# Two attention layers on one core: output products move to step 6, the first value products to step 7, and a weight copy moves between ScalarE's copy and VectorE's addition

## The chip, the core and the metric

The kernel runs on one core of a Trainium2 chip. The metric is the time of one execution on the device, in microseconds (us), lower is better. Before the change the median of three runs is 3574.42 us (3573.12 to 3576.17). The profiled execution has a span of 3577.0 us, with a granted TensorE clock of 0.994 of full speed, so throttling plays no part.

## What is computed

Four images of 32 x 32 positions with 768 channels go through two layers. Each layer normalizes in 32 groups, runs 12-head attention (head size 64) with decomposed relative position biases, projects, and adds the result to its input. All of it is fp32. Cut to one layer:

```
S = 32*32; hd = 64
q, k, v = split(groupnorm(x) @ Wqkv)              # 12 heads, [S, hd] each
bias    = rel_h[q_row, k_row] + rel_w[q_col, k_col]   # both are products of q with a small table
attn    = softmax(scale * q @ k.T + bias)         # [S, S] for each head and image
out     = (attn @ v) @ Wproj + bproj
x       = x + out
```

## The kernel before

**Pairs and steps.** Work is cut into 48 pairs of heads: 2 layers x 4 images make 8 images, each with 6 pairs (`pair` 0 to 5; the text counts pairs through, 0 to 47). A pair has 8 steps, `n` = 0 to 7, one for each block of 128 queries. The order of every engine's instructions is written out by hand in the main loop (L709 to L794): [...].

**What a step does.** In step n the loop issues, for the next block of queries, the score products (`scores`, L475 on TensorE: both heads, 1024 keys). VectorE then takes scores and bias together (L484) into a tile `sc`; ScalarE takes the exponential (L488). For the block of the step itself, already exponentiated, `turn` (L515) lets VectorE transpose 32 x 32 blocks into a tile `tb`. Then `divide` (L495, L499, L501) scales the next block by the inverse of its sums. GpSimd adds the two bias parts for the block after (L461).

**The way through DRAM.** Two steps fill one quarter of the queries. After each odd step SyncE writes `tb` to DRAM (`td<-tb`, L518, 1 MB for each head), and `read_back` (L526, `pt<-td`, 1 MB for each head) brings it back in the layout that the value products need. The first quarter (written in step 1) is read back in step 3, the second (step 3) in step 4, the third (step 5) in step 7, the fourth (step 7) in step 0 of the next pair. There are three `tb` buffers for the two heads together and two `pt` buffers for each head.

**Value products.** `weigh` (L545, `av<-pt,v`) multiplies two quarters with the values: quarters 0 and 1 in step 6 of the pair, quarters 2 and 3 in step 2 of the next pair. They need `pt` to have landed, and their end frees `pt` buffers.

**Filling work.** `take` hands out groups of matmuls that prepare the next pair or finish an earlier image: `project_in` (L268, four units a pair), `project_values` (L376), `project_out` (L621, four products a pair, three groups each). `shares` says how many groups each step takes. Before the change the four output products stand in step 7, and step 6 has no share, because the value products are there. An output product needs its weights (`wo`, L580) and the tile that it is added to (`res`, L600), which `fetch` loads half in step 4, half in step 6.

**PSUM.** All of the filling work, the position products (`tp`, L408) and the value products share one pool `ps_m` of two tiles. A product can start when the product two before it has been taken out of PSUM by VectorE or ScalarE. Scores have a pool of their own, one tile for each head.

**Saved products.** For pairs that are not `plain` (L237: the first pair of an image and pair 1 are plain) some products of `project_in` are saved with sums of weights: `sum_weights` (L318: one ScalarE copy L324, three GpSimd operations L327 to L329) runs in steps 6 and 7 two pairs ahead. In unit 0, `sum_weights_last` (L333) has VectorE overwrite part of `w0` (L336, 64x384) and GpSimd the rest (L337). Unit 1, three groups in step 1, reads what L336 wrote. `sum_input` (L339) prepares sums of the inputs on GpSimd in the last pair of each image.

**SyncE's queue.** Nearly all transfers are issued by SyncE, in order; [...]. In the built program each transfer also waits until the one eight before it has landed.

Of the kernel before, what the change touches and what calls it, by code (L numbers as in the profile page):

```python
# [52 lines left out]
NT = S // P  # L53
# [5 lines left out]
NP = NH // 2  # L59
FULL = 2 * HW - 1  # L60
BIG = 3.0e38
NX, NY = 2 * NC, NC + NC // 2
# [4 lines left out]
def attention_blocks(ctx: ExitStack, tc: tile.TileContext, a: dict, out: bass.AP):  # L67
# [28 lines left out]
    NPAIR = NI * NP  # L96
# [24 lines left out]
    def load_w(g, which):  # L121

        im, pair = divmod(g, NP)
        if which == 2:
            w = wpool.tile([P, NC, 2 * P], FP, tag="wv", name=f"wv_{g}")
            src = a[f"wv{images[im][0]}"][pair // 2]
        else:
            w = wpool.tile([P, NC, P], FP, tag=f"w{which}", name=f"w_{g}_{which}")
            src = a[f"wqk{images[im][0]}"][pair, which]
        w_of[g, which] = w  # L130
        nc.sync.dma_start(out=w, in_=src.rearrange("p (c o) -> p c o", c=NC))
# [105 lines left out]
    def plain(g):  # L237
        return g % NP == 0 or g == 1

    def add(to, t, x, bias=None):  # L240

        if bias is None:
            nc.vector.tensor_tensor(to, t, x, ALU.add)  # L243
        else:
            nc.vector.scalar_tensor_tensor(to, t, bias, x, ALU.add, ALU.add)

    def project_in(g, unit):

        im, pair = divmod(g, NP)
        xs, ys = x_of[im], y_of[im]  # L250
        if unit == 0:
            for which in range(2):
                tag = "qk"[which]
                qk_of[g, which] = qkpool.tile([P, S], FP, tag=tag, name=f"{tag}_{g}")
        if plain(g):
            which, i = divmod(unit, 2)
            w, x = 2 * [w_of[g, which]], xs[i * NC : (i + 1) * NC]
        else:
            w0, w1, w3 = w_of[g, 0], w_of[g, 1], w_of[g, 3]
            w, x = (  # L260
                ((w0, w0), xs[:NC]), ((w0, w3[:, 3:]), ys[NC:]),
                ((w3, w0), xs[NC:]), ((w1, w1), ys[:NC]),
            )[unit]
        t = ps_m.tile([P, 2, HALF], FP, tag="m", name=f"pj_{g}_{unit}")
        for c in range(len(x)):
            for a in range(2):
                rows = slice(a * D, (a + 1) * D)
                nc.tensor.matmul(  # L268
                    t[:, a, :], lhsT=w[a][rows, c, :], rhs=x[c][rows, :],
                    start=(c == 0), stop=(c == len(x) - 1),  # L270
                )
            if c < len(x) - 1:
                yield True

        q = [
            qk_of[g, 0][:, i * HALF : (i + 1) * HALF].rearrange("p (m a) -> p m a", a=4)
            for i in range(2)
        ]
        k = qk_of[g, 1].rearrange("p (a m) -> p a m", a=4)
        k = [k[:, :, i * P : (i + 1) * P] for i in range(2)]  # L280
        u = [t[:, a, :].rearrange("p (m a) -> p m a", a=4) for a in range(2)]
        t = [x.rearrange("p m a -> p a m") for x in u]
        bias = [None, None]
        if images[im][0]:
            bias = [bqkv[:, which, pair : pair + 1] for which in range(2)]
        if plain(g):
            to = k[i]
            if which == 0:
                to, t = q[i], u
            if images[im][0] == 0:  # L290
                nc.scalar.copy(to, t[0])
            else:
                nc.scalar.activation(to, t[0], AF.Identity, bias=bias[which])
            add(to, t[1], to)
        elif unit == 0:
            nc.scalar.copy(k[0], t[0])
            add(q[0], u[1], k[0].rearrange("p a m -> p m a"), bias[0])
            sum_weights_last(g)
        elif unit == 1:
            add(k[0], t[0], k[0])  # L300
            add(k[0], t[1], k[0])
        elif unit == 2:
            add(k[1], t[0], k[0])
            add(q[1], u[1], k[1].rearrange("p a m -> p m a"), bias[0])
        else:
            add(k[1], t[0], k[1], bias[1])
            add(k[0], t[0], k[0], bias[1])
            nc.vector.tensor_tensor(k[0], k[0], t[1], ALU.subtract)
        if unit in ((0, 1) if plain(g) else (0, 2)):
            (later if g else mid).append(lambda: positions(g, 1 if unit else 0))  # L310
        if g + 1 < NPAIR:
            if unit == (1 if plain(g) else 2):
                later.append(lambda: load_w(g + 1, 0))
            if unit == 3:
                early.append(lambda: load_w(g + 1, 1))
        yield True
# [16 lines left out]
    def sum_weights_last(g):  # L333

        w0, w3 = w_of[g, 0], w_of[g, 3]
        nc.vector.tensor_copy(w0[TOP, :3], w3[LOW, :3])  # L336
        nc.gpsimd.tensor_tensor(w0[LOW], w0[LOW], w3[LOW], ALU.subtract)  # L337

    def sum_input(im, n):  # L339

        xs, ys = x_of[im], y_of[im]

        def each(chunks):
            return [(c, xs[c], xs[NC + c], ys[c], ys[NC + c % 3], TOP if c < 3 else LOW) for c in chunks]

        sub = lambda out, x, y: nc.gpsimd.tensor_tensor(out, x, y, ALU.subtract)  # L346
        for c, a, b, y, z, half in each({-1: (0, 1, 2), 0: (3,), 1: (4,), 2: (5,)}.get(n, ())):
            nc.scalar.copy(y[LOW], b[TOP])  # L348
            sub(y[TOP], b[LOW], y[LOW])
        for c, a, b, y, z, half in each({1: (0,), 2: (1, 2), 3: (3,), 4: (4, 5)}.get(n, ())):  # L350
            nc.gpsimd.tensor_tensor(z[half], y[TOP], a[TOP], ALU.add)  # L351
            if half == TOP:
                nc.scalar.copy(y[LOW], z[TOP])
        for c, a, b, y, z, half in each({5: (0,), 6: (1, 2), 7: (3, 4, 5)}.get(n, ())):
            sub(b[TOP], b[TOP], a[TOP])
        for c, a, b, y, z, half in each({9: (0, 1, 2), 10: (3, 4, 5)}.get(n, ())):
            sub(y[LOW], (y if half == TOP else z)[LOW], a[LOW])
# [291 lines left out]
    early, mid, later, last, behind, behind2 = [], [], [], [], [], []  # L649
# [32 lines left out]
    with tc.manual_schedule(engines=ENGINES):  # L682
# [26 lines left out]
        for at, (g, n) in enumerate(units):  # L709
            im, pair = divmod(g, NP)  # L710
            end = im + 1 == NI
            if n == 0:
                shares = [6, 6, 0, 6, 12, 6, 0, 12] if g + 1 >= NPAIR or plain(g + 1) else [6, 9, 0, 6, 6, 6, 0, 12]
                ins = (todo if at == 0 else []) + prepare(g + 1)
                if pair < 3:
                    if at == 0:
                        shares = [12, 6, 0, 6, 12, 6, 0, 0]
                    todo = ins + (put_out(im - 1, 1, range(4 * pair, 4 * pair + 4)) if im else [])
                elif pair < NP - 1:
                    todo = ins + put_out(im, 0, range(4 * pair - 12, 4 * pair - 8))  # L720
                    if pair == 3 and not end:
                        stages, apply = norm(im + 1)
                else:
                    todo = ins + put_out(im, 0, range(8, 12))
                    if end:
                        fetch_last()
                        todo += put_out(im, 1, range(12)) + put_out(im, 2, range(0, 12, 2))
                        shares = [6, 6, 0, 6, 6, 2, 0, 4]
# [8 lines left out]
            early, later = later, early  # L737

            upto = 4 * (pair % 3) + 3
            if n in (4, 6) and (im, pair) >= (0, 3):  # L740
                upto -= 6 - n
                fetch(place[((im, 0) if pair >= 3 else (im - 1, 1)) + divmod(upto, 2)])

            ask = [divmod(g + 3, NP)] if n == 1 else []
# [14 lines left out]
            if pair == 3 and n in stages and not end:  # L759
                stages[n]()  # L760
            share = shares[n]
            first = 3 if n == NT - 1 else 2 if end and pair == NP - 1 and n in (3, 4) else 0
            first = min(first, share)
            take(todo, first)
            share -= first
# [1 line left out]
            if at + 1 < len(units):  # L767
                divide(*units[at + 1])
            if pair == 4 and not end:
                for c in {2: (0, 1), 4: (2, 3), 6: (4, 5, 6, 7), 7: range(8, NX)}.get(n, ()):  # L770
                    if n == 7 and c % 2 == 0:
                        take(todo, 3)
                        share -= 3
                    apply(c % NC, c // NC)
            if g + 2 < NPAIR and not plain(g + 2) and n in (6, 7):
                if n == 6:
                    combine = sum_weights(g + 2)
                combine[n - 6]()
            take(todo, share)
            if last:  # L780
                last.pop(0)()
            if pair == NP - 2 and n == 7 and not end:
                sum_input(im + 1, -1)
# [4 lines left out]
            elif g == 0:  # L788
                for k in (-1, 0) if n == 0 else (n,):
                    sum_input(0, k)  # L790
            if n == 6:
                weigh(g, (0, 1))
            elif n == 2 and g:
                weigh(g - 1, (2, 3))  # L794
# [62 lines left out]
```

## Time and profile before

| | before |
|---|---|
| time, median of 3 | 3574.42 us |
| TensorE (PE) busy | 3417.6 us, 96% |
| VectorE (DVE) busy | 2592.0 us, 72% |
| GpSimd (POOL) busy | 2492.1 us, 70% |
| ScalarE (ACT) busy | 1986.2 us, 56% |
| DMA, queue 1 | 1020.53 MB, 79.3% of 16 engines' span |
| one transposition on VectorE (L515) | 768 of 1222 ns |
| one output product's removal from PSUM (L632; L630) | 680 ns; 741 ns |
| weight copy on VectorE (L336) | 39 of 647 ns |
| ScalarE's copy of k in unit 0 (L296) | 39 of 566 ns |
| VectorE's addition of queries (L243 q; L245 q) | 38 of 1065 ns; 40 of 1121 ns |
| GpSimd weight sums (L327, L328, L329, L337) | 39 each of about 1805 ns |

The first rows are shares of the span; the lower rows are groups of instructions with their count and mean duration. The page also gives the time that an engine was idle just before a group, and what ended the idle time. TensorE's 3577.0 - 3417.6 = 159.4 us of idle time can thus be put down to what it waited for. A timeline lists one engine's instructions in order, with the start in us from the span's start, the time from the first start to the last end of a run of equal instructions, and in brackets the idle time before it with its releaser.

### The profile page before, as it was taken

What the parts mean: (1) busy time and instruction counts of PE and PEld (TensorE: products, weight loads), DVE (VectorE), ACT (ScalarE), POOL (GpSimd) and SP (SyncE); (2) the same over time, 40 slices, a digit from 0 to 9 for tenths busy, and PEclk for the clock granted to TensorE, in tenths of its full rate; (3) what the DMA queues carried; (4) which work ended last, traced back from release to release, by engine and by line L of the source; (5) the groups of instructions that cost most, each with busy time, mean ns of one, the idle gap of its engine ahead of it and who ended that gap; (6) DMA issues with size and microseconds to landing.
All of it is one profiled execution on the core that took longest, in us unless ns stands there. A gap on an engine that the chain in (4) does not pass through costs nothing.

```text
span 3577.0 us, 56189 instructions
## 1 busy us (share of the span) xinstructions
PE 3417.6 (96%) x20652; PEld 1897.0 (53%) x20652; DVE 2592.0 (72%) x4011; ACT 1986.2 (56%) x3958; POOL 2492.1 (70%) x1510
## 2 busy tenths in 40 slices
PE   6899999999999999999999999999999999999999
PEld 4455555555555556555555555555555555555554
DVE  4687867777777777777777777777766677776776
ACT  3565565555555556555655566555654555555552
POOL 3877686676967669676786667876678666786663
PEclk9999999999999999999999999999999999999999
DMA  3688978888788887888888788878988789887878
GB/s 118 244 287 319 328 278 302 318 309 316 276 316 317 300 307 272 319 293 306 292 308 304 281 316 301 306 285 292 308 307 301 271 290 330 299 291 276 296 288 289
DMA packets 531220, 1051.55 MB, mean 294 GB/s; under 512 B 143872, under 2 KB 206848, under 8 KB 481792
## 3 DMA queue, kind: packets, MB, share of 16 engines
q1 hardware_dynamic: 476448, 1020.53, 79.3%
q10 hardware_dynamic: 54496, 27.43, 2.6%
q8 instruction: 162, 2.65, 0.3%
q14 instruction: 114, 0.93, 0.1%
HBM read 572.73 MB, written 475.10 MB: 293 GB/s over the span
## 4 chain that ended last, share of the span: by engine, by line
PE 52%; DVE 17%; DMA 15%; ACT 5%; issue 5%; POOL 4%; SPq 2%; ACTq 0%; DVEq 0%; POOLq 0%
PE pj L268 13%; PE av L545 12%; PE s L475 10%; PE o L621 10%; DVE tb L515 8%; DMA td<-tb 7%; DMA pt<-td 7%; PE pv L376 6%; DVE sc L484 5%; ACT sc L501 2%; PE tp L408 2%; POOL sc L461 2%; DVE x L228 1%; POOL x L346 1%; POOL x L351 1%
## 5 line engine op out<-in xcount | busy, mean ns | idle before, releaser
L461 POOL TENSOR_TENSOR sc<-rel,rel 128x1024 f32<-128x1024 f32 x768 | 1546.1, 2083 | 42.6 <-DMA rel<-tdr 35.8
L488 ACT ACTIVATE sc<-sc,sm 128x1024 f32<-128x1024 f32 x768 | 880.1, 1147 | 662.8 <-DVE sm L484 660.0
L499 POOL TENSOR_SCALAR sc<-sc,sm 128x1024 f32<-128x1024 f32 x384 | 435.5, 1134 | 934.4 <-DVE sm L495 926.4
L484 DVE CUSTOM_DVE_ANT_0 sc<-s,sc 128x1024 f32<-128x1024 f32 x768 | 908.7, 1220 | 214.1 <-PE s L475 164.9
L268 PE MATMUL pj<-x,w 64*128 64x512 f32 x4140 | 938.7, 598 | 99.3 <-DVE w L336 60.1
L515 DVE STREAM_TRANSPOSE tb<-sc 128x1024 f32<-128x1024 f32 x768 | 913.0, 1222 | 122.9 <-DMA td<-tb 122.8
L545 PE MATMUL av<-pt,v 128*64 128x256 f32 x6144 | 717.3, 385 | 41.0 <-DMA pt<-td 41.0
L475 PE MATMUL s<-k,q 64*128 64x512 f32 x3072 | 746.3, 596 | 6.2 <-DVE sm L484 6.1
L501 ACT ACTIVATE sc<-sc,sm 128x1024 f32<-128x1024 f32 x384 | 441.0, 1148 | 556.8 <-DVE sm L495 556.8
L268 PEld LDWEIGHTS pj<-x,w 64*128 64x128 f32 x4140 | 415.7, 189 | 600.2 <-issue 444.4
L545 PEld LDWEIGHTS av<-pt,v 128*64 128x64 f32 x6144 | 446.0, 138 | 341.4 <-DMA pt<-td 60.3
L376 PE MATMUL pv<-wv,x 64*128 64x256 f32 x4608 | 514.1, 376 | 0.0
L376 PEld LDWEIGHTS pv<-wv,x 64*128 64x128 f32 x4608 | 446.4, 187 | 92.2 <-issue 29.9
L621 PE MATMUL o<-attn,wo 128*128 128x512 f32 x1080 | 480.5, 598 | 8.5 <-DVE attn L554 3.5
L475 PEld LDWEIGHTS s<-k,q 64*128 64x128 f32 x3072 | 289.2, 187 | 297.0 <-issue 272.7
L431 ACT COPY rel<-t 32x64 f32<-32x64 f32 x1504 | 362.9, 241 | 15.4
L621 PEld LDWEIGHTS o<-attn,wo 128*128 128x128 f32 x1080 | 199.9, 190 | 285.9 <-issue 234.4
L418 ACT COPY t<-tp 128x512 f32<-128x512 f32 x188 | 110.0, 585 | 191.5 <-PE tp L408 137.0
L243 DVE TENSOR_TENSOR k<-pj,k 128x512 f32<-128x512 f32 x173 | 116.8, 684 | 136.8 <-PE pj L268 94.9
L346 POOL TENSOR_TENSOR x<-x,x 64x512 f32<-64x512 f32 x144 | 182.6, 1288 | 43.9 <-ACT x L348 28.8
L391 DVE TENSOR_TENSOR v<-pv,v 128x256 f32<-128x256 f32 x192 | 81.4, 424 | 91.2 <-ACT v L388 88.0
L488 ACT ACTIVATION_READ_ACCUMULATOR sc<-sc,sm 128x1 f32 x768 | 143.2, 187 | 0.0
(54 smaller groups left out, 1516.9 us busy)
## 6 DMA issues: line engine op xcount, KB each, us to landing
td<-tb SPq DMA_DIRECT2D x384, 1024.0 KB, 5.6
pt<-td SPq DMA_DIRECT2D x382, 1024.0 KB, 8.0
w<-in_wqk SPq DMA_DIRECT2D x96, 384.0 KB, 3.5
tdr<-t ACTq DMA_DIRECT2D x94, 256.0 KB, 4.6
x<-in_x SPq DMA_DIRECT2D x84, 256.0 KB, 6.6
part<-res SPq DMA_DIRECT2D x84, 256.0 KB, 5.5
res<-part SPq DMA_DIRECT2D x84, 256.0 KB, 6.9
wv<-in_wv SPq DMA_DIRECT2D x24, 768.0 KB, 12.1
```

The lines of the kernel that those rows point to most:

```text
L268: nc.tensor.matmul(t[:, a, :], lhsT=w[a][rows, c, :], rhs=x[c][rows, :], start=(c == 0), stop=(c == len(x) - 1),)
L376: nc.tensor.matmul(t[:, a, k, :], lhsT=xs[i // 2 * NC + c][rows, at * P : (at + 1) * P], rhs=w[rows, c, :], start=(c == 0), stop=(c == NC ...
L431: nc.scalar.copy(rel[of, :, j, :], t[of, j, :, at : at + HW])
L461: nc.gpsimd.tensor_tensor(sc.rearrange("p (a k) (u l) -> p a l (k u)", a=4, l=8), rel0[:, h, :].unsqueeze(1).unsqueeze(2).to_broadcast(shape),
L475: nc.tensor.matmul(ps[h][:, cols], lhsT=q[rows, n * P : (n + 1) * P], rhs=k[rows, cols], start=True, stop=True,)
L484: nc.vector.tensor_tensor_reduce(out=sc, in0=ps[h], in1=sc, scale=-scale, scalar=BIG, op0=ALU.add, op1=ALU.min, accum_out=st[:, 0, h : h + 1],
L488: nc.scalar.activation(sc, sc, AF.Exp, bias=st[:, 0, h : h + 1], scale=-1.0, accum_out=st[:, 1, h : h + 1],)
L499: nc.gpsimd.tensor_scalar(sc, sc, st[:, 2, h : h + 1], 1.0, ALU.mult, ALU.mult)
L501: nc.scalar.activation(sc, sc, AF.Copy, scale=st[:, 2, h : h + 1])
L515: nc.vector.transpose(tb[:, :, j, :], sc_of[g, n, h])
L545: nc.tensor.matmul(av[rows, at * 2 * P : (at + 1) * 2 * P], lhsT=v_of[g][:, k, rows], rhs=pt_of[g, quarter, h][:, :, k, :], start=(k == 0) ...
L621: nc.tensor.matmul(t, lhsT=wo_of[im, o, c], rhs=attn_of[im * NP + c, i], start=(c == c0), stop=(c == c1 - 1),)
```

## The change

Three things move, and some timing around them is adapted.

1. In unit 0 of `project_in`, the weight copy (L336) and GpSimd's subtraction are issued before VectorE's addition of queries instead of after it, so that VectorE can do the copy while ScalarE still copies k.
2. The four output products move from step 7 to step 6; from pair 3 to pair 46 (`late`) the value products of quarters 0 and 1 move from step 6 to step 7. This gives the second quarter's read-back more time. `fetch` accordingly loads both `wo` tiles and all four `res` tiles in step 5.
3. `sum_weights` runs one step earlier (5 and 6) unless the next pair is plain; two rows of the position bias copies (`rows_axis`, L431) are allowed in step 3; the normalization of the next image's inputs (`apply`, L228) is spread differently over the steps of pair 4; `sum_input` is one step earlier in places.

```diff
         elif unit == 0:
             nc.scalar.copy(k[0], t[0])
+            sum_weights_last(g)
             add(q[0], u[1], k[0].rearrange("p a m -> p m a"), bias[0])
-            sum_weights_last(g)
...
-        for c, a, b, y, z, half in each({5: (0,), 6: (1, 2), 7: (3, 4, 5)}.get(n, ())):
+        for c, a, b, y, z, half in each({5: (0, 1), 6: (2, 3, 4, 5)}.get(n, ())):
...
-                shares = [6, 6, 0, 6, 12, 6, 0, 12] if g + 1 >= NPAIR or plain(g + 1) else [6, 9, 0, 6, 6, 6, 0, 12]
+                shares = [6, 6, 0, 6, 12, 6, 12, 0] if g + 1 >= NPAIR or plain(g + 1) else [6, 9, 0, 6, 6, 6, 12, 0]
+                late = g > 2 and g + 1 < NPAIR
...
-            if n in (4, 6) and (im, pair) >= (0, 3):
-                upto -= 6 - n
+            if n == 5 and (im, pair) >= (0, 3):
                 fetch(place[((im, 0) if pair >= 3 else (im - 1, 1)) + divmod(upto, 2)])
...
-            first = 3 if n == NT - 1 else 2 if end and pair == NP - 1 and n in (3, 4) else 0
+            first = 3 if n == (6 if late else 7) else 2 if end and pair == NP - 1 and n in (3, 4) else 0
...
-                for c in {2: (0, 1), 4: (2, 3), 6: (4, 5, 6, 7), 7: range(8, NX)}.get(n, ()):
-                    if n == 7 and c % 2 == 0:
+                for c in {2: (0, 1), 3: (2,), 4: (3,), 5: (4,), 6: range(5, 10), 7: (10, 11)}.get(n, ()):
+                    if n == 6 and c % 2 == 0:
...
-            if g + 2 < NPAIR and not plain(g + 2) and n in (6, 7):
-                if n == 6:
+            if g + 2 < NPAIR and not plain(g + 2):
+                k = n - (6 if plain(g + 1) else 5)
+                if k == 0:
                     combine = sum_weights(g + 2)
-                combine[n - 6]()
+                if k in (0, 1):
+                    combine[k]()
...
-            if last:
+            for k in range(min(len(last), 2 if n == 3 else 1)):
                 last.pop(0)()
...
-            if n == 6:
+            if n == (7 if late else 6):
                 weigh(g, (0, 1))
```

## The prediction

> **What bounds the kernel now.** I read the shares first: TensorE is busy in 96% of the span, VectorE in 72%. So only TensorE's gaps can be won, and any delay elsewhere counts only where TensorE comes to wait for it. Its waits name the gaps (us in total, times, longest):
>
> ```profile
> PE pj L268 <- DVE w L336: 60.1, 39, 4.4
> PE av L545 <- DMA pt<-td: 41.0, 34, 2.7
> PE pj L268 <- DVE x L228: 25.8, 1, 25.8
> ```
>
> The third is the start. The first two are what the change goes for. Next, TensorE's timeline over pair 19's steps 6 and 7 and pair 20's steps 0 and 1; each step begins with a row of L475:
>
> ```profile
> 1498.71 1.88 PE L475 MATMUL s<-k,q 64*128 64x512 f32 x8
> 1500.52 7.13 PE L545 MATMUL av<-pt,v 128*64 128x256 f32 x64
> 1507.58 1.99 PE L475 MATMUL s<-k,q 64*128 64x512 f32 x8
> 1509.50 10.57 PE L621 MATMUL o<-attn,wo 128*128 128x512 f32 x24
> 1519.99 1.99 PE L475 MATMUL s<-k,q 64*128 64x512 f32 x8
> 1521.82 5.32 PE L268 MATMUL pj<-x,w 64*128 64x512 f32 x24
> 1526.96 1.88 PE L475 MATMUL s<-k,q 64*128 64x512 f32 x8
> 1530.21 8.00 PE L268 MATMUL pj<-x,w 64*128 64x512 f32 x36 [1.36 <-DVE w L336]
> ```
>
> Unhindered, step 6 takes 1507.58 - 1498.71 = 8.87 us, step 7 12.41, step 0 6.97; step 1 has 1.36 us of waiting (11.97 between score starts in this pair, 10.6 without). Read the same way for every pair, the surplus is: **step 1**, 48.2 us over the 36 non-plain cases from pair 4 on, and 10.7, 6.7, 6.9 us in pairs 1 to 3; **step 6**, 35.5 us over the 29 pairs at places 0 to 3 of an image (1.2 each), 35.7 us over the eight pairs at place 4, nothing at place 5; **step 7** of place 4, 12.6 us over seven. Together about 156 us. At place 4 the surplus is partly inside rows called busy (pair 22):
>
> ```profile
> 1719.93 0.65 PE L545 MATMUL av<-pt,v 128*64 128x256 f32 x2 [0.29 <-DMA pt<-td]
> 1722.69 5.26 PE L545 MATMUL av<-pt,v 128*64 128x256 f32 x30 [2.11 <-DMA pt<-td]
> ```
>
> Thirty of these take 3.67 us when nothing holds them. Last, what else happens in step 6 (pair 19; SPq issues transfers):
>
> ```profile
> 1491.95 0.43 SPq L580 DMA_DIRECT2D wo<-in_wo  x1
> 1492.47 0.85 SPq L600 DMA_DIRECT2D res<-part  x2
> 1493.38 0.97 SPq L526 DMA_DIRECT2D pt<-td  x2
> 1497.98 1.46 SPq L518 DMA_DIRECT2D td<-tb  x2
> ```
>
> and VectorE in the same step:
>
> ```profile
> 1504.09 1.24 DVE L515 STREAM_TRANSPOSE tb<-sc 128x1024 f32<-128x1024 f32 x1
> 1506.59 1.25 DVE L515 STREAM_TRANSPOSE tb<-sc 128x1024 f32<-128x1024 f32 x1 [1.26 <-DMA td<-tb]
> ```
>
> VectorE's second transposition of step 6 needs a `tb` buffer that the write of step 5 still reads. It waits for that in nearly every pair (`DVE tb L515 <- DMA td<-tb`, 122.8 us, of which 39 waits with 120.3 us lie in step 6), and begins 9.2 us after the step's start on average at places 0 to 2. Today little on TensorE hangs on it, since value products leave no PSUM tile to be emptied before they end.
>
> [...] what is issued behind `pt` lands behind it: `wo` takes 6.0 us in the median, and up to 13.7.
>
> **The change, part by part.**
>
> *Weight copy.* Today, after unit 0, VectorE waits 1.69 us for ScalarE (which first does L501, 1.15), adds queries (1.03 at 1528.52), then copies (0.57 at 1529.58). Moved ahead, the copy can follow the reciprocal at 1526.70 as soon as unit 0's products end (1527.14); it would be done near 1527.8, before TensorE wants it at 1528.84. By itself: 1.36 us a pair won, 48.2 in all. What could eat this is the reciprocal, which stands in front; see *step 0*.
>
> *Step 6 takes the output products.* TensorE's plan: scores to 1.84 us after the step's start, then four products of 10.57/4 = 2.64 us; the fourth starts at 9.77 and uses the PSUM tile of the second. On VectorE the second's removal stands behind both transpositions, the reciprocal and the first removal. If the second transposition starts at 9.1, it ends at 10.35, the reciprocal (0.12) and the removal (0.69 to 0.75) at 11.3: TensorE waits 11.3 - 9.77 = 1.5 us, a new wait in the place of the old. At odd places ScalarE also takes the weight copy L324 (0.83) before the value copies that VectorE waits for (1.47 at pair 19), and in layer 0 statistics (0.69) come in front of the transpositions: up to 2.2.
> Does `td` land earlier? `pt` of quarter 1 is issued about 1.4 us earlier (ahead of `wo` and `res`), but all 1.4 MB of `wo` and `res` now stand between it and `td`, where 0.7 MB stood ahead of it before. At the 365 GB/s that this stretch moves, the extra 0.7 MB costs 1.9 us; the earlier issue gives back 1.4. So `td` lands within about half a microsecond of today. By the same queue `wo` lands only after both halves of `pt`: an estimate of 2.5 to 3.5 us after the step's start, while the first product wants it at 1.84. This second new wait overlaps the first and rarely adds. I take **1.7 us** for places 0 to 3 (bounds 0.4 if `td` lands 1.5 us earlier, 2.7 if 1 us later).
>
> *Place 4.* `pt` and `td` are later there (VectorE's transposition begins at 11.2 on average), and one `apply` (0.69) stands before the second removal: 11.2 + 1.25 + 0.12 + 0.69 + 0.75 = 14.0, a wait of 4.0 (bounds 1.5, 5.5). Against this stand 35.7 and 12.6 us today: the wait for `pt` is gone, and step 7's wait on VectorE too, as the applies now come in between products. Place 5: 0.3, its `td` lands by 6.7.
>
> *Value products in step 7.* Quarter 1's `pt` has 12 us more: the 41.0 us wait ends. The third quarter's `pt` cannot be issued before quarter 0's products end, 1.9 + 3.7 = 5.6 us into step 7, where it used to be issued in step 6; it is wanted in step 2, more than 20 us on, and lands in 8.0: hidden. But step 7's two writes `td` queue behind it.
>
> *Step 0.* VectorE's second transposition there needs the first of these writes. 2 MB of `pt` land 5.2 (least time seen) to 8 us plus 2.6 after 5.7, the write 2.6 later: 16.1 us or more after step 7's start. VectorE wants it at 8.87 + 2.1 + 2.4 + 1.2 = 14.6. A wait of 1.5 to 1.9 us is new there (before, step 7 was 3.54 us longer and the write 5 us earlier). The reciprocal comes at 17.7, the weight copy at 18.4, TensorE wants it at 8.87 + 6.97 + 1.9 = 17.75: **0.65 us** remain of 1.36 (bounds 0 and 1.5).
>
> *Sums of weights.* One step earlier on GpSimd: 5.4 us in a step of 12.4 that has 5.2 of its own; hidden, as the bias tile behind it is wanted 10.9 us into step 7. It ends the late copies of pairs 2 and 3 (6.7 and 6.9 to 0.65 each); pair 1's stays, its weights being summed where they were. The added copies of step 3 (2.0 us on ScalarE) delay VectorE by about 0.6 at odd places, inside the 2.2 above. `sum_input` a step earlier: hidden by the longer step 6.
>
> *Sum.* Step 1: 48.2 - 36 x 0.65 = 24.8 won; pairs 2 and 3: 12.3 won; places 0 to 3: 29 x 1.7 - 35.5 = 13.8 lost; place 4: 48.3 - (7 x 4.0 + 1.4) = 18.9 won; place 5: 2.1 lost. 40.1 won of 3574.4: **3534 us**.
>
> **Rivals.** *All waits go* (A). If `td` lands early in both places, 0.4 remains at places 0 to 3 (23.9 won), 1.5 at place 4 (37), nothing in step 1 (48.2), 13 in pairs 2 and 3: 122 won, 3452 us. For it: `pt` leaves earlier, and nothing follows `td` in the queue. Against it: 39 waits today under a lighter load ahead of `td`. *New waits outweigh the old* (B). 2.7 at places 0 to 3 (42.8 lost), 5.5 at place 4 (8 won), 1 at place 5 (7 lost), 1.5 in step 1 (6 lost), 12 won in pairs 2 and 3: 36 lost, 3610 us. For it: the load ahead of `td`, the late `wo`, DMA at 0.98 of its time here. Against it: the waits overlap each other.
>
> **How the numbers follow.** Likeliest case 55%, A 18%, B 27%. An error of 0.7 us in each of 29 steps and 0.5 in 36 moves the likeliest by 20 and 18 us, so some of it ends within 0.2% (7 us) or slower. Faster: 0.48 + 0.18 + 0.03 = 0.69; within: 0.08; slower: 0.23. The range 3468 to 3603 leaves out half of A and a third of B.
>
> **What would show it.** TensorE's waits lose `pt<-td`, keep `DVE w L336` at 0.3 to 1 us, and gain one on the removal (`res`) before the fourth output product and one on `wo` before the first. VectorE's `tb` waits appear in step 0 as well as step 6. It would be wrong if step 6 ran its 12.41 us unhindered (A), or if value products in step 2 came to wait for the fourth quarter.

## The result, and the profile after

The changed kernel takes **3704.06 us** (median of 4 runs, 3698.35 to 3706.17) against 3574.94 us (4 runs, 3573.12 to 3576.17): ratio 1.0359, 95% interval 1.0341 to 1.0377. That is 129 us slower. The prediction said 3534 us; its range ended at 3603.

The page of the kernel after has this row of busy times, in a span of 3704.4 us:

```profile
PE 3465.2 (94%) x20652; PEld 1942.2 (52%) x20652; DVE 2573.0 (69%) x4011; ACT 1990.5 (54%) x3958; POOL 2495.1 (67%) x1510
```

TensorE is idle for 3704.4 - 3465.2 = 239.2 us, 80 more than before. It is also *busy* for 48 us more, with the same 20652 matmuls: some of them became longer. Both parts have to be explained. This is what TensorE waited for (us in total, times, longest):

```profile
PE o L621 <- DMA wo<-in_wo: 89.8, 37, 6.1
PE pj L268 <- DVE w L336: 66.9, 39, 7.2
...
PE av L545 <- DVE q L243: 18.9, 7, 2.8
...
PE o L621 <- DVE res L632: 3.0, 5, 0.9
PE av L545 <- DMA pt<-td: 1.6, 1, 1.6
```

The wait for `pt` is gone but for 1.6 us (41.0 us before), as intended. The weight copy, which the change was to bring forward, is waited for as often as before, and longer (60.1 us before). The largest wait, which was 0.6 us before, is the one for the weights of the output products. In the list of waits of all engines, VectorE's waits for a `tb` buffer went from 122.8 us to

```profile
DVE tb L515 <- DMA td<-tb: 152.5, 67, 4.4
```

In program order, 134.1 of these 152.5 us belong to the second transposition of step 0, which had no such wait before, and only 16.3 to step 6 (120.3 before).

Now pair 20 of the kernel after, steps 6 and 7, on TensorE's timeline:

```profile
1629.26 1.88 PE L475 MATMUL s<-k,q 64*128 64x512 f32 x8
1633.48 12.09 PE L621 MATMUL o<-attn,wo 128*128 128x512 f32 x24 [2.33 <-DMA wo<-in_wo]
1645.50 1.99 PE L475 MATMUL s<-k,q 64*128 64x512 f32 x8
1647.42 7.13 PE L545 MATMUL av<-pt,v 128*64 128x256 f32 x64
```

The four output products start 2.33 us late, and take 12.09 us for 10.57. What SyncE issued around it:

```profile
1622.53 1.92 SPq L526 DMA_DIRECT2D pt<-td  x2
1624.49 1.22 SPq L580 DMA_DIRECT2D wo<-in_wo  x2
1625.81 2.36 SPq L600 DMA_DIRECT2D res<-part  x4
1630.26 3.05 SPq L518 DMA_DIRECT2D td<-tb  x2
```

`wo` stands behind 2 MB of read-back. The first of its two tiles lands 3.6 to 3.9 us after the start of step 6 on average at places 0 to 3, at place 4 6.1 us, and is wanted at 1.84. Before, `wo` landed 2.7 us ahead of the step. The first write `td` that is issued in this step lands at 9.7 us on average, against 9.0 before (both at places 0 to 3).

Then step 7 and step 0 of the next pair, first SyncE, then VectorE, then TensorE:

```profile
1651.12 1.02 SPq L526 DMA_DIRECT2D pt<-td  x2
1652.19 1.17 SPq L518 DMA_DIRECT2D td<-tb  x2
```

```profile
1662.71 1.25 DVE L515 STREAM_TRANSPOSE tb<-sc 128x1024 f32<-128x1024 f32 x1 [2.57 <-DMA td<-tb]
1663.88 0.12 DVE L495 RECIPROCAL sm<-sm 128x2 f32<-128x2 f32 x1
1664.03 0.35 DVE L336 COPY w<-w 64x384 f32<-64x384 f32 x1
```

```profile
1661.45 1.88 PE L475 MATMUL s<-k,q 64*128 64x512 f32 x8
1664.44 8.30 PE L268 MATMUL pj<-x,w 64*128 64x512 f32 x36 [1.11 <-DVE w L336]
```

The read-back is issued in front of the two writes; the first write lands 33.35 us after step 6 began (17.1 after step 7 began). VectorE's 4011 instructions and SyncE's 1886 transfers start in program order in this trace, and in all 39 cases the copy stands directly behind the two transpositions and the reciprocal. So VectorE's second transposition, the reciprocal and the weight copy behind it are late, and TensorE, which waits for it in front of step 1's products, waits for the copy in its new place too.

I sum, for every step from pair 3 on, the time from its first score product to the next step's, less the unhindered length (10.6 us for step 1, as in the prediction; 12.3 for step 6 of the kernel after, the shortest seen). This surplus (us in all pairs together) shows where the 129 us are:

| step | before | after |
|---|---|---|
| 1 (weight copy) | 55.1 | 90.6 |
| 2 (33.7 after at place 5) | 0.2 | 34.8 |
| 3 (only place 4) | 0 | 8.0 |
| 6 | 71.1 | 133.3 |
| 7 | 12.8 | 0.2 |

The differences add up to 128. In step 1, `e1_copy_only` below shows steps of 10.33 us, so that 10.6 is 0.27 too long and a surplus can come out below 0. The 8 us of step 3 begin with three waits, 5.1 us in all, of `project_in` for VectorE to take value products out of PSUM (L554, L557); which part of the change causes them stays open.

**Why matmuls became longer.** The granted clock of the kernel after is 0.979 in the mean, before 0.994. In stretches of pair 20 (from:to, length, TensorE, weight loads, VectorE, ScalarE, GpSimd, granted clock, DMA share, GB/s), the gap before the output products, the 3.4 us behind it, and the rest of the step:

```profile
1629.30:1633.40 4.10, 1.85 (x10) 0.55 (x6) 3.72 (x7) 2.82 (x3) 4.04 (x3) 0.97 1.05 379
1633.50:1636.90 3.40, 3.40 (x5) 1.56 (x6) 0.16 (x2) 1.44 (x4) 0.94 (x1) 0.55 1.04 425
1636.90:1645.50 8.60, 8.60 (x21) 3.54 (x20) 6.45 (x10) 1.15 (x1) 3.70 (x3) 1.00 0.73 301
```

For most of the 3.4 us after the gap TensorE runs at half clock: three products take 1061 to 1220 ns and a fourth 787, the later ones 592. The mean of the page hides such stretches, since all 40 slices still read 9. This was so before too, in fewer places: the value products of pair 22 that took 5.26 us for 3.67 had a clock of 0.52 in their first 3.4 us. So throttling did play a part before the change: its trace has 13 stretches at half clock, that of the kernel after 39. TensorE is busy for 41.1 us in the former and for 136.5 us in the latter. Half of the difference is 47.7 us, which is the 48 us of longer matmuls.

### The profile page after: what moved, and what is told of

It reads as the page before. It is cut to its first block, busy times and chain, and to the rows that moved or that the text cites. A ratio compares the mean times of both kernels' runs of the same rounds, so it can differ in the third digit from the quotient of the medians.

```text
span 3704.4 us, 56289 instructions
## 1 busy us (share of the span) xinstructions
PE 3465.2 (94%) x20652; PEld 1942.2 (52%) x20652; DVE 2573.0 (69%) x4011; ACT 1990.5 (54%) x3958; POOL 2495.1 (67%) x1510
## 4 chain that ended last, share of the span: by engine, by line
PE 36%; DMA 26%; DVE 14%; ACT 9%; issue 6%; POOL 5%; SPq 4%; ACTq 0%; DVEq 0%; POOLq 0%
DMA td<-tb 16%; PE o L621 12%; PE pj L268 10%; DVE tb L515 7%; PE av L545 6%; DMA wo<-in_wo 6%; PE s L475 6%; DVE sc L484 4%; POOL sc L461 3%; SPq L447 3%; ACT rel L431 2%; ACT sc L488 2%; ACT sc L501 2%; PE tp L408 2%; PE pv L376 1%
## 5 line engine op out<-in xcount | busy, mean ns | idle before, releaser
L499 POOL TENSOR_SCALAR sc<-sc,sm 128x1024 f32<-128x1024 f32 x384 | 444.3, 1157 | 1057.2 <-DVE sm L495 1028.4
L268 PE MATMUL pj<-x,w 64*128 64x512 f32 x4140 | 958.5, 606 | 106.0 <-DVE w L336 66.9
L515 DVE STREAM_TRANSPOSE tb<-sc 128x1024 f32<-128x1024 f32 x768 | 916.8, 1225 | 153.1 <-DMA td<-tb 152.5
L268 PEld LDWEIGHTS pj<-x,w 64*128 64x128 f32 x4140 | 452.3, 192 | 590.2 <-issue 387.7
L475 PE MATMUL s<-k,q 64*128 64x512 f32 x3072 | 754.0, 599 | 7.1 <-DVE sm L484 6.9
L545 PE MATMUL av<-pt,v 128*64 128x256 f32 x6144 | 696.7, 385 | 20.5 <-DVE q L243 18.9
L621 PE MATMUL o<-attn,wo 128*128 128x512 f32 x1080 | 509.1, 627 | 96.8 <-DMA wo<-in_wo 89.8
L621 PEld LDWEIGHTS o<-attn,wo 128*128 128x128 f32 x1080 | 210.0, 200 | 395.5 <-issue 244.7
L431 ACT COPY rel<-t 32x64 f32<-32x64 f32 x1504 | 363.3, 242 | 16.5
L391 DVE TENSOR_TENSOR v<-pv,v 128x256 f32<-128x256 f32 x192 | 81.5, 424 | 110.7 <-ACT v L388 107.6
```

What stands on the lines that cost most here:

```text
L268: nc.tensor.matmul(t[:, a, :], lhsT=w[a][rows, c, :], rhs=x[c][rows, :], start=(c == 0), stop=(c == len(x) - 1),)
L431: nc.scalar.copy(rel[of, :, j, :], t[of, j, :, at : at + HW])
L475: nc.tensor.matmul(ps[h][:, cols], lhsT=q[rows, n * P : (n + 1) * P], rhs=k[rows, cols], start=True, stop=True,)
L499: nc.gpsimd.tensor_scalar(sc, sc, st[:, 2, h : h + 1], 1.0, ALU.mult, ALU.mult)
L515: nc.vector.transpose(tb[:, :, j, :], sc_of[g, n, h])
L545: nc.tensor.matmul(av[rows, at * 2 * P : (at + 1) * 2 * P], lhsT=v_of[g][:, k, rows], rhs=pt_of[g, quarter, h][:, :, k, :], start=(k == 0) ...
```

## The experiments

Theories on the swap are told apart here; the expectations speak of them in their own words. **Q, order in SyncE's queue:** what the swap of output and value products does to the order of transfers costs the time. **V, order on VectorE:** in step 6 the second product's removal stands behind transpositions that wait for `td`, and the fourth product for it. **B, bandwidth:** something waits for the same bytes in whatever order they are moved. In the expectations of `e2_swap_only` and `e3_no_swap`, theory 1 is that the swap alone makes the loss, and theory 2 that the copy or the sums have a share in it; in that of `e4_wo_early`, theory 1 is Q and theory 2 is V. Each kernel was timed beside the kernel before; ratios are against that.

### One part alone: the copy, the swap, all but the swap

`e1_copy_only` is the kernel before with the copy in its new place:

```diff
+            sum_weights_last(g)
             add(q[0], u[1], k[0].rearrange("p a m -> p m a"), bias[0])
-            sum_weights_last(g)
```

> The kernel before, with only the weight copy moved ahead of the addition of queries. Both theories: the 1.36 us wait of step 1 goes, since nothing delays the reciprocal in step 0 here: 48 us in 36 pairs, 3527 us, ratio 0.987. If the reciprocal or ScalarE were the real limit in step 1, less than half of that.

Measured: 3531.88 us, ratio 0.9864 (0.9849 to 0.9879). Step 1's surplus fell from 55.1 to 6.1 us. The copy by itself is worth what the prediction put on it, though not pair by pair: step 1 kept its 1.24 us at place 0, and elsewhere 1.6 us each were won.

`e2_swap_only` is the kernel after with the old place of the copy and the old timing of the sums:

```diff
+            add(q[0], u[1], k[0].rearrange("p a m -> p m a"), bias[0])
             sum_weights_last(g)
-            add(q[0], u[1], k[0].rearrange("p a m -> p m a"), bias[0])
...
-        for c, a, b, y, z, half in each({5: (0, 1), 6: (2, 3, 4, 5)}.get(n, ())):
+        for c, a, b, y, z, half in each({5: (0,), 6: (1, 2), 7: (3, 4, 5)}.get(n, ())):
...
-            if g + 2 < NPAIR and not plain(g + 2):
-                k = n - (6 if plain(g + 1) else 5)
-                if k == 0:
+            if g + 2 < NPAIR and not plain(g + 2) and n in (6, 7):
+                if n == 6:
...
```

> The changed kernel with the copy behind the addition and the sums of weights (and of inputs) as before, so the swap of steps 6 and 7 alone, with its loads. Theory 1, the swap alone makes the loss: slower than the changed kernel, since the wait in front of the reciprocal in step 0 stays and the copy comes 1.7 us of waiting and 1.05 us of addition later: 36 x 2.5 = 90 us more in step 1, about 3790 us. Theory 2, the copy or the sums cause part of the loss: at or below 3704 us.

Measured: 3857.97 us, ratio 1.0779 (1.0761 to 1.0797), worse than expected. TensorE waits 4.6 us for the copy in step 1 on average, but the surplus there, over steps of 10.33 us, is 7.0 us a pair: 2.4 us are in no wait. The trace puts 2.2 of these on stretches at half clock.

`e3_no_swap` is the kernel before with copy, earlier sums of weights and earlier sums of inputs:

```diff
+            sum_weights_last(g)
             add(q[0], u[1], k[0].rearrange("p a m -> p m a"), bias[0])
-            sum_weights_last(g)
...
-        for c, a, b, y, z, half in each({5: (0,), 6: (1, 2), 7: (3, 4, 5)}.get(n, ())):
+        for c, a, b, y, z, half in each({5: (0, 1), 6: (2, 3, 4, 5)}.get(n, ())):
...
-            if g + 2 < NPAIR and not plain(g + 2) and n in (6, 7):
-                if n == 6:
+            if g + 2 < NPAIR and not plain(g + 2):
+                k = n - (6 if plain(g + 1) else 5)
+                if k == 0:
...
```

> The kernel before with the moved copy, the earlier sums of weights and the earlier sums of inputs, without the swap. Theory 1 (loss from the swap alone): 48 us and 12 us in pairs 2 and 3 won, 3514 us, ratio 0.983. Theory 2 (GpSimd's earlier sums hurt): not better than the copy alone.

Measured: 3509.88 us, ratio 0.9808 (0.9793 to 0.9823), close to what theory 1 expected. So these parts of the change win 71 us of the 3580.65 that the kernel before took beside it, and **the swap, with the fetch, applies and rows that go with it, loses all that and 129 us more**.

### Step 6: two waits, one behind the other

`e4_wo_early` lets `fetch` load both `wo` in step 4 and `res` in step 5:

```diff
-            if n == 5 and (im, pair) >= (0, 3):
-                fetch(place[((im, 0) if pair >= 3 else (im - 1, 1)) + divmod(upto, 2)])
+            if n in (4, 5) and (im, pair) >= (0, 3):
+                fetch(place[((im, 0) if pair >= 3 else (im - 1, 1)) + divmod(upto, 2)], n == 5)
```

The second argument says whether `res` is loaded too.

> The changed kernel with both wo tiles fetched in step 4, ahead of quarter 1's read-back; res stays in step 5. Theory 1, order in SyncE's queue: the 89.8 us wait on wo goes, and with it the half-speed clock after those gaps; the second product's removal then sets step 6, at 1 to 2 us: 40 to 80 us faster than the changed kernel, 3625 to 3665 us. Theory 2, the removal behind the transposition sets step 6 anyway and the wait on wo only overlaps it (as my prediction had it): within 15 us of 3704.

Measured: 3749.41 us, ratio 1.0474 (1.045 to 1.0498): 45 us slower than the kernel after, which neither theory expected. The wait for `wo` is gone, and TensorE's waits now have the removals:

```profile
PE o L621 <- DVE res L632: 54.4, 25, 2.9
PE o L621 <- DVE res L630: 42.7, 19, 4.4
```

The fourth product waits, as the prediction had it. `td` lands 1.0 us later than in the kernel after (10.7 us), so the wait is longer, and it comes in one piece: 2.84 us in pair 20, with slow matmuls behind it (six in 4.54 us for 2.64):

```profile
1649.00 4.54 PE L621 MATMUL o<-attn,wo 128*128 128x512 f32 x6 [2.84 <-DVE res L632]
```

So in the kernel after the wait for `wo` had only hidden the wait for the removal. The late first product delays its own removal, and with it the transpositions that VectorE does behind it, so that these seldom find `td` missing: step 6 has 16.3 us of `tb` waits in the kernel after, and 73.5 in `e4_wo_early`. `f1_two_first` undoes the other one: in step 6 two products are issued ahead of the transpositions, so that VectorE removes both first.

```diff
-            first = 3 if n == (6 if late else 7) else 2 if end and pair == NP - 1 and n in (3, 4) else 0
+            first = (6 if late else 3) if n == (6 if late else 7) else 2 if end and pair == NP - 1 and n in (3, 4) else 0
```

> The changed kernel with the second output product of step 6 also taken from PSUM before the two transpositions. Theory V (VectorE's order: a removal stands behind a transposition that waits for td): the fourth product no longer waits, but the first still waits for wo (89.8 us and slow clock after it, of a step 6 surplus of 133), so only 15 to 35 us faster than the changed kernel: 3670 to 3690 us. Theory Q (queue order alone, wo): no change, 3704 us.

Measured: 3697.73 us, ratio 1.0338 (1.0318 to 1.0357): 6 us better than after, whose interval it overlaps, and less than theory V expected. The wait for `wo` stays at 82.4 us. `f2_wo_two_first` does both:

> The same, and wo fetched in step 4 as in e4_wo_early. Theory V: both waits of step 6 are gone, its surplus of 180 us in e4 falls under 20: about 3585 us. Theory Q: as e4, about 3750 us. Theory B (bandwidth: something in step 6 waits for the same bytes whatever the order): above 3680 us, with a new wait in step 6, on res.

Measured: 3637.62 us, ratio 1.0163 (1.0146 to 1.018): 66 us better than after, less than expected. Step 6 keeps 57.7 us of surplus, 47 of them at places 3 and 4 (3 us each). **Neither repair of step 6 pays alone, both together do**: two waits in series on one path.

### Step 7: the writes behind the read-back

`f3_td_first` issues the two writes of step 7 ahead of the read-back of the third quarter, and changes nothing else in the kernel after:

```diff
-            run(behind)
-            behind, behind2 = behind2, behind
+            held, behind, behind2 = behind, behind2, []
+            if n != NT - 1:
+                run(held)
...
             turn(g, n)
+            run(held)
```

> The changed kernel with the write td of step 7 issued ahead of the read-back of the third quarter. Theory Q: VectorE's tb wait of step 0 goes, with it the surplus of step 1 (90.6 us) and that of step 2 at place 5 (34 us): 110 to 125 us faster, about 3585 us. Theory B: the read-back then lands later and TensorE waits for it in step 2: no faster than 3680 us.

Measured: 3591.69 us, ratio 1.0037 (1.0025 to 1.0049), 112 us better than after, as expected. Its waits on TensorE hold the first two lines below; the third is from the waits of VectorE:

```profile
PE o L621 <- DMA wo<-in_wo: 84.5, 34, 6.3
...
PE pj L268 <- DVE w L336: 9.3, 3, 6.1
```

```profile
DVE tb L515 <- DMA td<-tb: 15.4, 14, 2.6
```

Step 1's surplus is -5.7 us for 90.6, that of step 2 2.3 for 34.8, with nothing left at place 5; step 6 keeps 140.8. So one order of two transfers was behind both step 1 and step 2. At place 5 of the kernel after the link is again VectorE: its second transposition in step 0 waits (4.27 us in pair 23), its additions of queries come later, and in step 2 the value products wait for a PSUM tile that such an addition empties.

`f4_all_three` takes all three repairs:

> All three: wo in step 4, two removals before the transpositions, td ahead of the read-back. Theories V and Q together: the 272 us of surplus fall to 20 to 40: 3455 to 3480 us, faster than the kernel before and than the copy and sums alone (3510 us). Theory B: above 3575 us.

Measured: 3537.11 us, ratio 0.9883 (0.9868 to 0.9898). It is faster than before, but 57 us over the slow end of what I expected, and behind `e3_no_swap`: repaired, the swap still costs 27 us. The rest is in step 6 (56.0 us), where TensorE's longest waits are for VectorE (`DVE v L391` 16.6 us, `DVE res L630` 15.8), and in step 2 (20.0). I didn't follow it further, so the cause of this rest stays open.

### Does the gap make the slow clock?

That a half clock follows a gap was read from traces; both might come from a third thing, such as transfers. So I filled gaps with spare matmuls whose results are overwritten: work is added, and nothing is released earlier. `g1_fill_step6` (on the kernel after) and `g2_fill_step1` (on `e2_swap_only`) fill in front of the waiting product, in the PSUM tile that it takes. This is g2; g1 has 8 in step 6 of the pairs that are `late`, and 18 at place 4:

```diff
+        if unit == 1 and not plain(g):
+            q, k = qk_of[g - 1, 0], qk_of[g - 1, 1]
+            for r in range(16):
+                rows = slice((r % 2) * D, (r % 2 + 1) * D)
+                nc.tensor.matmul(
+                    t[:, r % 2, :], lhsT=q[rows, :P], rhs=k[rows, :HALF], start=True, stop=True
+                )
```

> The kernel after with spare score products (64x512, 235 ns each, results overwritten) put on TensorE in step 6 in front of the first output product, in the PSUM tile that this product takes: 8 of them (1.9 us), 18 at place 4 (4.2 us). They fill the time in which TensorE waits for wo and release nothing else. Theory 'the slow clock follows a gap': after a gap of about 2 us or more TensorE runs 3.4 us at half speed, 32.6 us of long output products in step 6 in all. The gaps shrink to under 1 us at most places, the long products (1061 ns for 592) go nearly everywhere, and 10 to 25 us are won although work is added: 3680 to 3694 (not all of 32.6, because the fourth product then waits longer for its PSUM tile). Theory 'the products are long because transfers are landing meanwhile': they stay long, and the time stays at 3704 or rises by up to 10 us where the filling is longer than the gap.

> e2_swap_only with 16 spare score products (3.8 us, results overwritten) on TensorE in front of unit 1 in step 1, where TensorE waits 4 to 6.5 us for the weight copy in 39 cases and then runs its next products at half speed in nearly all. Theory 'the slow clock follows a gap': the gaps shrink to 0.5 to 2 us, the slow stretch (3.4 us at half speed, 1.7 us each) goes in most of the 39, some 45 to 65 us won: 3793 to 3813. Rival: the long products come from something else that happens then (VectorE and transfers): 3858, within 10 us.

Measured: g1 3747.25 us, ratio 1.0482 (1.0468 to 1.0496); g2 3843.93 us, ratio 1.0745 (1.0728 to 1.0762). No output product over 700 ns is left in g1 (76 in the kernel after), and those of `project_in` fell from 438 in `e2_swap_only` to 40 in g2. But both kernels were slower than expected, and g1 is slower than the kernel after. The fillings were twice as long as I had meant, since each such product is two instructions on TensorE, of 225 ns each in g1: 3.6 and 7.0 us, which then set the length of the step themselves. So the clock's part of the time couldn't be read from them. With half the filling:

> g1_fill_step6 with half the filling: each spare product turned out to be two instructions of 225 ns, so that g1 filled 3.6 us (8.1 at place 4), more than most gaps for wo, and set the length of step 6 itself (3.4 us of surplus everywhere), although not one long output product was left. Here 4 products (1.8 us), 9 at place 4 (4.0 us), again with overwritten results. Theory 'the slow clock follows a gap': gaps of 0.3 to 1 us remain, no long products, and step 6 of the kernel after (133 us of surplus) shrinks by 10 to 30 us: 3675 to 3695. Rival, that filling cannot win because the wait is only moved: 3700 to 3715.

> g2_fill_step1 with 9 spare products (4.0 us) for 16 (7.0 us, which was the whole length of the gap and of the slow stretch behind it, so little was won). TensorE waits 4.5 us on average in step 1 of e2_swap_only, and the surplus there is 7.0 us a pair: the 2.5 above the wait are the slow clock by the theory 'the slow clock follows a gap'. The gap is then under 1 us, the surplus 4.5 to 5, and 60 to 90 us are won against 3858: 3768 to 3800. Rival, that something else makes the products long: 3845 to 3860.

Measured: g3 3698.04 us, ratio 1.0345 (1.0329 to 1.0361); g4 3764.11 us, ratio 1.0531 (1.0505 to 1.0556). **g4 is 94 us faster than `e2_swap_only` although some 4 us of work on TensorE are added in each of 39 pairs.** The same place on TensorE's timeline, first of `e2_swap_only`:

```profile
1722.88 9.51 PE L268 MATMUL pj<-x,w 64*128 64x512 f32 x36 [4.32 <-DVE w L336]
```

then of g4, where added lines move L268 to L275:

```profile
1674.02 4.45 PE L269 MATMUL pj<-k,q 64*128 64x512 f32 x18
1678.80 8.00 PE L275 MATMUL pj<-x,w 64*128 64x512 f32 x36 [0.33 <-DVE w L343]
```

and the granted clock (third number from the end) in the 3.4 us from the first waiting product on, in `e2_swap_only`:

```profile
1722.90:1726.30 3.40, 3.40 (x10) 1.58 (x12) 3.40 (x5) 2.18 (x3) 3.40 (x2) 0.55 0.92 327
```

and in g4:

```profile
1678.80:1682.20 3.40, 3.40 (x16) 1.66 (x18) 3.40 (x5) 2.16 (x3) 3.40 (x2) 1.00 0.96 302
```

DMA, VectorE and ScalarE are as busy in one as in the other; only the gap is gone, and with it the half clock. From pair 3 on, the clock falls to half in step 1 of all 37 pairs that have this wait in `e2_swap_only`, and of 2 in g4. The surplus of step 1 falls from 252 to 174 us; most of the other 16 us are in step 6, which the filling did not touch. That the gap is the cause of the slow clock is thus shown. In the kernel after the gain is small: g3 is 6 us faster, within the spread, and lies between what the theory and its rival expected. Its step 6 shows why. At places 0 to 4 the surplus falls from 132 to 119 us (the half-clock stretches of step 6 from 16 to 2); at place 5, where there was hardly a gap, the filling itself costs 11.

### A version that beats both

`e7_pt_first` is `e3_no_swap` with `fetch` in steps 4 and 6 behind the read-backs, so that the second quarter's `pt` is issued ahead of `wo` and `res`:

```diff
-            if n in (4, 6) and (im, pair) >= (0, 3):
-                upto -= 6 - n
-                fetch(place[((im, 0) if pair >= 3 else (im - 1, 1)) + divmod(upto, 2)])
...
             run(behind)
             behind, behind2 = behind2, behind
+            if n in (4, 6) and (im, pair) >= (0, 3):
+                upto -= 6 - n
+                fetch(place[((im, 0) if pair >= 3 else (im - 1, 1)) + divmod(upto, 2)])
```

> e3_no_swap (3510 measured, 66 us of surplus left in step 6) with fetch in steps 4 and 6 issued behind the read-backs, not ahead of them, so that the second quarter's pt is issued ahead of wo and res in step 4. Theory 'order in the queue': pt lands 1.5 to 2.5 us earlier in step 6, the wait of the value products for it (38.0 us) ends at places 0 to 3 and shrinks at place 4, about 25 to 40 us won: 3470 to 3485. Rival: pt is held by the bandwidth or by the tb wait of step 5, not by what is issued ahead of it: 3505 to 3515.

Measured: **3479.25 us**, ratio 0.9733 (0.9719 to 0.9747), as expected from the order in the queue. The second half of `pt` lands 3.3 us after the start of step 6, for 6.2 in `e3_no_swap`, at places 0 to 3; `wo` lands about as late as in the kernel after (3.7 to 4.1 us), but is wanted only in step 7. TensorE's waits:

```profile
PE o L621 <- DVE attn L557: 15.5, 4, 5.6
PE o L621 <- DVE attn L554: 14.6, 4, 5.4
...
PE av L545 <- DMA pt<-td: 2.1, 4, 0.9
```

At places 0 to 3 the surplus of step 6 went from 29.8 us to 0. At place 4 the wait only moved: 36.2 us in step 6 became 3.8, and 12.9 in step 7 became 45.0, where output products wait for VectorE to take value products out of PSUM.

## Why the prediction was wrong

**The bound** was read rightly: TensorE's gaps set the time. The 80 us more of gaps and the 48 us of slow matmuls behind them make up the 127 us between the two spans. **The signs of the waits** came true in part: `pt` lost, waits on `wo` before the first output product, `tb` waits in step 0 (134.1 us) as well as step 6 (16.3). The wait on the removal hardly shows (`res` L632, 3.0 us), and that for the weight copy is longer than the 0.3 to 1 us forecast. The likeliest case failed by one overlap taken the wrong way round (step 6), a term too small (step 0) and two missing terms (step 2, slow clock), all on the side of its rival B, which at 3610 was still too low.

- *Weight copy*, "1.36 us a pair won, 48.2 in all": the sum is right, by itself 48.8 us (3580.65 - 3531.88), but two errors cancel in it: nothing was won at place 0, and 1.6 us each elsewhere.
- *Step 6*, "This second new wait overlaps the first and rarely adds": this failed. `wo` landed at 3.6 to 3.9 us, not 2.5 to 3.5, and TensorE waits 55.5 / 29 = 1.9 us for it at places 0 to 3. It is the first wait that shows, and the fourth product's is hidden behind it. The sum of 1.7 us was near the wait by accident; the surplus is 81.3 / 29 = 2.8, and about half of the other 0.9 is slow clock (13.3 us in 29 pairs).
- *Place 4*, "a wait of 4.0": priced from the removal alone. TensorE waits 4.3 us for `wo`, and the surplus is 50.7 / 8 = 6.3 with the slow clock, against 29.4 us in all in my sum. Had I taken the landing of `wo` there from the later `pt`, I'd have had it.
- *Value products in step 7*: `pt`'s wait ended, and the third quarter's read was hidden, as said. That the writes queue behind it was said too, but priced at 0.65 us a pair; it is worth 112 us (`f3_td_first`).
- *Step 0*, "0.65 us remain of 1.36": mis-sized. The sum took the least landing seen, 5.2 us, and 2.6 for the second MB (2.7 in the median of the kernel before). In pair 20 both MB of `pt` had landed only 9.0 us after the first was issued, not 7.8, and the write 17.1 us after step 7 began, not 16.1 (17.6 on average). The wait was 1.56 us on average from pair 3 on and the surplus 2.2 to 2.9 a pair: 90.6 us for the 23 of the sum.
- *Step 2 at place 5*: no term. The late `tb` delays VectorE through steps 0 to 2 and costs 4.8 us seven times. I asked who waits for the copy behind the transposition, not for what stands behind the copy.
- *Slow clock*: no term. I took the mean clock of 0.994 as "no part", and priced each wait at its length. Half of TensorE's 136.5 us of busy time at half clock, 68 us, were lost to it in the kernel after, and 21 before.
- *Sums of weights*, "It ends the late copies of pairs 2 and 3 (6.7 and 6.9 to 0.65 each)": this failed too. They are 5.1 and 2.0 us in the kernel after, and 5.2 and 5.3 in `e3_no_swap`. `e3_no_swap`, which has the sums of inputs too, is 22 us faster than `e1_copy_only`, for 12.3 in my sum, but this is luck: 10.6 of them are in step 1 at place 0, and under 3 in pairs 2 and 3.

By step, measured surplus less the predicted one: step 1 67, step 6 at places 0 to 3 32, place 4 21, step 2 35, step 3 8: 163 of the 170 us between 3534 and 3704. Another 4 are the late copy of pair 2.

## What to carry to other kernels

When work is moved to another step, write down the order of the transfers that it turns round and follow each one that is now further back, to all that is queued behind its user. Two waits in series hide each other: repair one alone and the time may not move, or get worse. And an idle gap on TensorE can cost more than its length: step 1 of `e2_swap_only` lost 7.0 us a pair for 4.6 of waiting. In the counts below slow matmuls follow 12 of 181 gaps of 1 to 2 us, and 69 of 70 of over 3 us.

## What was not expected of the hardware

After a gap on TensorE the granted clock can be half for 3.41 us (0.55 in the windows above), or for twice that (28 of the 65 stretches in `e2_swap_only`), which cost 1.5 us in pair 20 and 2.2 us a pair in step 1 of `e2_swap_only`. In the traces of the kernels before and after, `e2_swap_only`, `e4_wo_early` and g4, from pair 3 on, slow matmuls followed 12 of 181 gaps of 1 to 2 us, 34 of 57 of 2 to 2.5, 39 of 57 of 2.5 to 3, and 69 of 70 longer ones. So at 2 to 3 us it varied, with 73 of 114. Most of the stretches in the kernels before and after, 42 of 52, are 3.41 us long.

A read-back was not passed by what was issued behind it. In the kernel after, 230 writes `td` were issued while the last read-back ahead of them had not landed, and all landed after it, by 2.4 to 9.5 us; so did all 88 `wo` issued in this way, by 0.5 to 3.5 us (before: 175 `td`, by 2.4 to 6.7 us, and 45 `wo`, by 5.4 to 7.2). VectorE's waits for `tb` fell from 152.5 to 15.4 us by issuing the writes of step 7 first, with the same transfers.
